# A rewritten beginning: the first image fetched on three queues ahead of the weights, its norm by matrix products, and the first strip's values first

## The chip, the cores and the metric

The kernel runs on one core of one Trainium2 chip. A core has five engines with a queue of instructions each: TensorE (PE; its weight loads are shown apart as PEld), VectorE (DVE), ScalarE (ACT), GpSimd (POOL) and SyncE (SP). SyncE, ScalarE and GpSimd issue DMA transfers. The metric is the device time of one execution in microseconds; it is given as the median over runs.

## The reference

The input x holds 16 images of 56 x 56 tokens with 384 channels, in float32. Two layers are computed, each added to its input:

```
x = x + window_attention(group_norm(x))
x = x + depthwise_conv3x3(group_norm(x), sign of the clipped weights)

group_norm(v):  32 groups of 12 channels; mean and variance over height, width and the
                channels of a group, per image; (v - mean) / sqrt(var + 1e-5)
window_attention(x):
    roll x by (-3, -3); q, k, v = split(x @ w_qkv.T); 12 heads of 32
    windows of 7 x 7 = 49 tokens; score = q k / sqrt(32) + relative position bias
    mask across the rolled border in the last row and column of windows
    softmax over the 49 keys; out = attn v, then @ w_out.T + b_out; roll back
```

So every image needs its whole group norm before the first window of it can be computed.

## The kernel before, in words

An image is cut into 8 strips of 7 rows (NS = 8), a strip into 8 windows, and a unit is half a strip, 4 windows. There are 128 strips and 256 units. Channels lie on the 128 partitions, in three chunks (NC = 3). For a unit, `scores` (L527) makes the products of keys and queries in four banks of PSUM, `softmax` (L550) scales them and adds the bias, `exponential` (L573) takes the exponential, `add_up` (L604) sums over the keys with a product of ones, `attend` (L622) makes the products with the values, `invert` and `divide` normalize, and `project` (L662) makes the output product and adds the input. For the next strip, `value` (L483) and `query_key` (L471) make the products with the weights from the normalized input `xn`, which `normalize` (L460) writes on ScalarE. `turn` (L496) transposes blocks of the values on VectorE, and `by_key` (L505) carries them to their places with 16 DMAs on SyncE. The first product of `add_up` in a strip waits for these carries.

The order of the work on each engine is the order in which the program issues it. `all_units` (L985) is the loop over the units: in it, `heavy` gives the products for the next strip, and the list `side`, filled by `plan`, gives the work of other images with a due time in units: image b + 1 is loaded on GpSimd's queue during image b (`fetch_halves` L409, `turn_halves` L437, `arrange` L442), and the convolution of image b - 1 runs on VectorE.

The beginning is written out by hand (L1032 to L1060). It concerns image 0 only:

- `clear` (L133) zeroes the tails of the staging buffers on GpSimd. Two of the buffers are `xls`; four more are borrowed from the tiles `es`, `xn`, `vt`, `vq` (the list `spare`, L128).
- `fetch` (L371) loads a strip by 6 DMAs (12 for the last strip, which wraps around the image), all on SyncE's queue. A token's 384 channels are one row of 1536 bytes. The strip's two parities of rows are fetched apart, and each of them as 48, 5 and 3 tokens, because of the roll. Strips 0 to 5 go to the six buffers at once, strips 6 and 7 to `xls` again when these are free.
- `fetch_weights` (L154) loads `w_qkv` and `w_out` by 12 DMAs on ScalarE's queue, at the same time.
- `load_bias` (L192) gathers the relative position bias by 49 row DMAs on GpSimd's queue, 38 of them early and 11 after the norm's power, then a copy of the rows and two DMAs of the mask.
- `load` (L386) transposes a strip on TensorE, ScalarE copies it into `xs`, and VectorE takes its statistics. `load_weights` (L163) transposes 3 x 3 blocks of a weight (n = 0 query, 1 key, 2 value, 3 output); of its three copies out of PSUM two are on VectorE, one on ScalarE. Weights 0, 1 and 2 are turned after strips 3, 5 and 7.
- `norm_gather` (L240) aggregates the statistics per channel, writes them to DRAM and reads them back with a group on each partition; `clear_again` (L148) zeroes `es`, `xn`, `vt` and `vq` on VectorE; `norm_scale` (L255) folds the 12 channels of a group by small VectorE operations, takes the power -0.5 on GpSimd (L281), writes to DRAM and reads the coefficients back per channel.
- The output weight, `load_depthwise` (L173, the sign of the convolution's weights by six operations and a transpose) and `add_bias` (L221, sixteen additions of bias and mask) follow, then `normalize(0)` and `all_units`, which begins with the first strip's queries and keys, scores, softmax, values, turns and carries.

The norm of the last image's second layer is another function, `norm_late` (L323): there the means over a group are products with the matrix `gmat` (seven of its 128 x 128 blocks), which `fetch_late` loads.

If a value leaves its range, a second, slower pass is computed (`tc.If(redo != 0)`); it is not entered with these inputs.

Of the kernel before, what the change touches and what calls it, by code (L numbers as in the profile page):

```python
# [9 lines left out]
F32 = mybir.dt.float32  # L10
# [8 lines left out]
EPS = 1e-5  # L19
# [15 lines left out]
def kernel(  # L35
# [97 lines left out]
    def clear():  # L133
        for xl in xls:
            nc.gpsimd.memset(xl[:, NL - 1, :], 0.0)

        for t in spare:
            nc.gpsimd.memset(t[:, NL - 1, :], 0.0)

    def clear_more():  # L140
        nc.gpsimd.memset(power, -0.5)
        nc.gpsimd.memset(ones, 1.0)
        nc.gpsimd.memset(least, LEAST)
        nc.gpsimd.memset(seen, 0.0)
        for t in (qk[:, :, ST:], *hps, *accs):
            nc.gpsimd.memset(t, 0.0)
# [5 lines left out]
    staged = []  # L152

    def fetch_weights():  # L154

        rows = [w[r * P : (r + 1) * P, :] for w in (w_qkv, w_out) for r in range(w.shape[0] // P)]
        for n in range(0, len(rows), NC):
            wl = xpool.tile([P, NC, ST], F32, tag="x", name=f"wl_{n}")
            for k in range(NC):
                nc.scalar.dma_start(wl[:, k, :C], rows[n + k])  # L160
            staged.append(wl)
# [10 lines left out]

    def load_depthwise():  # L173
        wl = [accs[1].rearrange("p h w -> p (h w)")[:9, n * C : (n + 1) * C] for n in range(3)]
        nc.scalar.dma_start(wl[0], w_dw.rearrange("a b c o -> (a b) (c o)"))
        for c in range(NC):
            nc.scalar.dma_start(bo_sb[:, c : c + 1], b_out[c * P : (c + 1) * P].unsqueeze(1))

# [144 lines left out]
    def norm_late(b):  # L323
        st, gm = stats.pop((1, b)), late_tiles["gm"]
        mv = small.tile([P, NC, 2], F32, tag="mv", name="mv_late")
        for c in range(NC):
            nc.vector.bn_aggr(mv[:, c, :], st[:, c].rearrange("p s k -> p (s k)"))
        nc.vector.tensor_tensor(mv[:, :, 0], mv[:, :, 0], bo_sb, ALU.add)
# [17 lines left out]
        mean = group_mean(mv[:, :, 0], "pg_mean")  # L346
        dev = small.tile([P, 3, NC], F32, tag="dev_late", name="dev_late", bufs=1)
# [4 lines left out]
        var = seen[:, B : B + NC]  # L352
        nc.vector.tensor_scalar(var, group_mean(dev[:, 0], "pg_var"), EPS, None, ALU.add)
        nc.gpsimd.tensor_tensor(dev[:, 1], var, power.to_broadcast([P, NC]), ALU.pow)
        coef = small.tile([P, NC, 2], F32, tag="coef", name="coef_late", bufs=4)
        nc.vector.tensor_copy(coef[:, :, 0], dev[:, 1])
        nc.vector.scalar_tensor_tensor(coef[:, :, 1], dev[:, 2], -1.0, dev[:, 1], ALU.mult, ALU.mult)
        coefs[1, b] = coef

    xs = {}

    def staging(s):

        if NS > s >= 2 and s < 2 + len(spare) and staged:
            return spare[s - 2]
        return xls[s % 2]

    def fetch(s):  # L371
# [3 lines left out]
        for odd in range(2):  # L375
            t, end = 0, (WIN + 1 - odd) // 2
            while t < end:
# [4 lines left out]
                for lo, hi in ((SHIFT, SHIFT + 48), (SHIFT + 48, W), (W, R)):  # L382
                    nc.sync.dma_start(here[lo - SHIFT : hi - SHIFT], rows[lo % W : (hi - 1) % W + 1])
# [495 lines left out]
    def plan_last(b, first):  # L879
# [6 lines left out]
        at(first, norm_late, b)  # L886
# [98 lines left out]
    def all_units(fast):  # L985
        for m in range(2 * NC):
            query_key(0, m)
        scores(0, fast)
        softmax(0, fast)
        for m in range(NC):  # L990
            value(0, m)
        normalize(1)
        exponential(0, fast)
        for m in range(NC):
            turn(0, m)
        by_key(0)
# [35 lines left out]
    with tc.manual_schedule():  # L1032
        nc.scalar.preload_act_table_set("natural_log_exp_and_others")
        clear()
        nc.vector.memset(score_banks, 0.0)
        staged.append(None)
        for s in range(2 + len(spare)):
            fetch(s)
        staged.clear()
        fetch_weights()  # L1040
        clear_more()
        load_bias(nc.gpsimd, 0, 38, True)
        for s in range(NS):
            for c in range(NC):
                load(s, c)
            if s + 2 + len(spare) < NS:
                fetch(s + 2 + len(spare))
            if s % 2 and s > 1:
                load_weights(s // 2 - 1)
        norm_gather((0, 0), nc.sync)  # L1050
        clear_again()
        for xl in xls:
            nc.gpsimd.memset(xl, 0.0)
        norm_scale((0, 0), nc.sync, nc.vector)
        load_bias(nc.gpsimd, 38, T, True)
        load_weights(NC)
        load_depthwise()
        add_bias(True)
# [81 lines left out]
```

## Time and profile before

| what | us |
|---|---|
| median of 3 runs | 4051.73 (4049.64 to 4053.24) |
| the profiled execution's own time | 4050.03 |
| its span, first to last instruction | 4048.2 |
| TensorE busy | 3948.1 (98%) |
| VectorE busy | 3495.5 (86%) |
| ScalarE busy | 2227.4 (55%) |
| GpSimd busy | 1858.7 (46%) |
| last strip of image 0 lands (its transposes start) | 39.49 |
| its last statistics end | 42.89 |
| first query product starts | 59.38 |
| products with the values of unit 0 end | 94.67 |

The profile is one execution. "L474" is line 474 of the program. A line of the timeline or the chain begins with the start and the length in microseconds; a group names its engine, its line and its tiles, written from read, and at the end the idle time of the engine before it and what ended that. "PEclk" is the clock granted to TensorE as a share of full speed. DMA share is the mean busy share of the core's 16 DMA engines. The span is 1.8 us shorter than the execution's own time.

### The profile page before, as it was taken

How to read it: one execution, taken by the hardware profiler on the slowest of the kernel's cores; microseconds unless marked ns; L12 is line 12 of the kernel's file. 1: busy time of each engine (PE TensorE's matmuls, PEld its weight loads, DVE VectorE, ACT ScalarE, POOL GpSimd, SP SyncE). 2: the span in 40 equal slices, each digit the busy share in tenths (PEclk: the TensorE clock that was granted, in tenths of full speed). 3: DMA queues.
4: the chain of work that ended last, by engine and by line, in shares of the span. 5: the costliest groups of instructions: out<-in, count | busy, mean ns of one | idle time of the engine just before them, and what ended most of it. 6: DMA issues, size and time to landing. Idle time of an engine off the chain costs nothing.

```text
span 4048.2 us, 144624 instructions
## 1 busy us (share of the span) xinstructions
PE 3948.1 (98%) x63161; PEld 2408.9 (60%) x63161; DVE 3495.5 (86%) x3712; ACT 2227.4 (55%) x4654; POOL 1858.7 (46%) x3165
## 2 busy tenths in 40 slices
PE   5999999999999999999999999999999999999987
PEld 3656555555566565555655656565555556556657
DVE  4555989889898998989889898998989899898897
ACT  2545655555565655655555565655556556565552
POOL 5444535545463554545446453554545455452100
PEclk8999999999999999999999999999999999999998
DMA  3323445454554554445454454554545454553444
GB/s 96 81 60 93 112 101 128 109 113 98 120 115 112 118 117 104 114 99 128 108 117 109 111 118 106 118 119 101 118 101 123 106 126 104 112 120 80 114 100 107
DMA packets 803093, 438.90 MB, mean 108 GB/s; under 512 B 672538, under 2 KB 753083, under 8 KB 802450
## 3 DMA queue, kind: packets, MB, share of 16 engines
q1 hardware_dynamic: 711784, 267.66, 30.4%
q0 software_dynamic: 87648, 159.12, 15.7%
q8 instruction: 498, 8.16, 0.9%
q10 hardware_dynamic: 3018, 2.78, 0.3%
q14 instruction: 145, 1.19, 0.1%
HBM read 169.63 MB, written 158.46 MB: 81 GB/s over the span
## 4 chain that ended last, share of the span: by engine, by line
PE 33%; issue 22%; POOL 18%; DVE 16%; DMA 8%; ACT 2%; SPq 1%; DVEq 0%; ACTq 0%; POOLq 0%
POOL xl L421 13%; PE pq L474 13%; PE pv L487 7%; PE py L671 7%; DVE o L799 6%; PE score_banks L541 2%; PE po L632 2%; DMA mvd<-mv 2%; DVE xt L438 2%; DVE e L558 2%; DMA xl<-in_x_dram 2%; PE score_banks L611 1%; POOL dev L270 1%; SPq L511 1%; DMA cod<-both 1%
## 5 line engine op out<-in xcount | busy, mean ns | idle before, releaser
L474 PE MATMUL pq<-xn,wq_t 128*128 128x392 f32 x4608 | 1586.8, 497 | 0.2 <-issue 0.2
L421 POOL DMA_DIRECT2D xl<-in_x_dram x1980 | 1329.2, 729 | 143.9 <-DVE xt L438 96.9
L799 DVE SCALAR_TENSOR_TENSOR o<-hp,dw_t,o 128x1568 f32<-128x1568 f32 x752 | 1379.1, 1834 | 5.4
L474 PEld LDWEIGHTS pq<-xn,wq_t 128*128 128x128 f32 x4608 | 846.1, 188 | 596.2 <-issue 1.8
L487 PE MATMUL pv<-xn,wq_t 128*128 128x392 f32 x2304 | 814.6, 497 | 15.2 <-DVE y L679 14.0
L671 PE MATMUL py<-ot,wo_t 128*128 128x392 f32 x2304 | 817.6, 500 | 8.4 <-DVE ot L660 7.8
L481 ACT COPY qk<-pq 128x392 f32<-128x392 f32 x768 | 367.2, 482 | 565.6 <-PE pq L474 565.2
L691 POOL COPY y<-y 128x63 f32<-128x63 f32 x128 | 54.7, 427 | 1276.7 <-DVE y L679 1276.7
L487 PEld LDWEIGHTS pv<-xn,wq_t 128*128 128x128 f32 x2304 | 423.6, 188 | 314.9 <-DVE y L679 16.2
L671 PEld LDWEIGHTS py<-ot,wo_t 128*128 128x128 f32 x2304 | 424.8, 190 | 312.0 <-DVE ot L660 27.1
L576 ACT ACTIVATE e<-e 128x1176 f32<-128x1176 f32 x256 | 303.3, 1185 | 495.9 <-DVE e L558 494.8
L652 DVE SCALAR_TENSOR_TENSOR ln<-score_banks,inv 128x588 f32<-128x588 f32 x256 | 196.0, 766 | 321.7 <-ACT inv L651 317.6
L494 ACT COPY vt<-pv 128x392 f32<-128x392 f32 x384 | 188.8, 492 | 367.6 <-PE pv L487 366.8
L558 DVE SCALAR_TENSOR_TENSOR e<-score_banks,bias 128x1176 f32<-128x1176 f32 x256 | 347.3, 1357 | 8.7 <-PE score_banks L541 8.7
L541 PEld LDWEIGHTS score_banks<-qk 32*49 32x49 f32 x24576 | 265.8, 118 | 145.9 <-issue 113.0
L632 PEld LDWEIGHTS po<-e,v 49*32 49x32 f32 x24576 | 311.8, 105 | 58.7 <-issue 8.2
L450 ACT COPY x<-xt 128x196 f32<-128x196 f32 x720 | 225.6, 368 | 180.8 <-DVE xt L438 180.7
L632 PE MATMUL po<-e,v 49*32 49x49 f32 x24576 | 311.0, 212 | 7.2 <-DMA v<-vq 7.0
L541 PE MATMUL score_banks<-qk 32*49 32x49 f32 x24576 | 298.2, 218 | 3.1 <-DVE ln L652 3.0
L498 DVE STREAM_TRANSPOSE vq<-vt 128x512 f32<-128x512 f32 x384 | 266.1, 694 | 8.6 <-ACT vt L494 5.5
L463 ACT ACTIVATE xn<-x,coef 128x392 f32<-128x392 f32 x384 | 247.0, 711 | 13.2 <-DMA coef<-cod 13.2
L679 DVE TENSOR_TENSOR y<-py,x 128x392 f32<-128x392 f32 x384 | 213.6, 556 | 42.1 <-PE py L671 41.6
(174 smaller groups left out, 3281.7 us busy)
## 6 DMA issues: line engine op xcount, KB each, us to landing
v<-vq SPq DMA_DIRECT2D x2048, 48.0 KB
xb<-mid SPq DMA_DIRECT2D x90, 855.5 KB
out_dram<-o SPq DMA_DIRECT2D x736, 98.0 KB
mid<-y POOLq DMA_DIRECT2D x112, 619.5 KB
xl<-in_x_dram POOLq DMA_DIRECT2D x1260, 52.5 KB
mid<-y POOLq DMA_DIRECT2D x15, 354.0 KB
xl<-in_x_dram POOLq DMA_DIRECT2D x180, 28.0 KB
mid<-y POOLq DMA_DIRECT2D x15, 265.5 KB
```

The source lines that it names most:

```text
L421: nc.gpsimd.dma_start(xz[i * D + lo : i * D + hi, c, k : k + n, :], flat[token : token + n * (hi - lo)].rearrange("(k t) c -> t k c", k=n) ...
L463: nc.scalar.activation(xn[:, c, :, :T], xs[s][:, c, :].rearrange("p (w t) -> p w t", t=T), AF.Identity, bias=coef[:, c, 1:2], scale=coef[: ...
L474: nc.tensor.matmul(pq[:, :ST].rearrange("p (w t) -> p w t", t=T), wq_t[:, c, m * P : (m + 1) * P], xn[:, c, :, :T], start=(c == 0), stop=( ...
L481: nc.scalar.copy(qk[:, m, :ST], pq[:, :ST])
L487: nc.tensor.matmul(pv[:, :ST].rearrange("p (w t) -> p w t", t=T), wq_t[:, c, 2 * C + m * P : 2 * C + (m + 1) * P], xn[:, c, :, :T], start= ...
L498: nc.vector.transpose(vq[:, :, :, m].rearrange("p h n d -> p n h d"), vt[:, m].rearrange("p (n w) (j b) -> p n (w j) b", w=2, b=D),)
L541: nc.tensor.matmul(pp[row * HT : row * HT + rows, i, k0 : k0 + T], qk[part, NC * fast + j, q0 : q0 + rows], qk[part, NC * (not fast) + j, ...
L558: nc.vector.scalar_tensor_tensor(e, pp[:, :, : NC * 2 * T].rearrange("q i (n k) -> q i n k", k=T), QSCALE, bias[:, int(s % NS == NS - 1)]. ...
L576: nc.scalar.activation(flat, flat, AF.Exp, accum_out=reach[:, 0, u : u + 1])
L632: nc.tensor.matmul(po[w][i * D : (i + 1) * D, (2 * j + r) * T : (2 * j + r + 1) * T], vs[s][keys, i, n * 2 + r, j], by_head(u)[keys, i * N ...
L671: nc.tensor.matmul(py[:, :ST], wo_t[:, c, m * P : (m + 1) * P], ots[s][:, c, :], start=(c == 0), stop=(c == NC - 1),)
L799: nc.vector.scalar_tensor_tensor(acc, by_half(hp[:, dy : dy + BR, dx : dx + W]), dw_t[:, c, t : t + 1], acc, ALU.mult, ALU.add)
```

## The change

It rewrites the beginning.

1. *Buffers and clears.* Two more staging buffers are borrowed from the tiles of `by_key` (`vpool`), so each of the eight strips has its own; the tails are cleared on VectorE (`make_room`). The clears of `es`, `xn`, `vq` and most of `vt` are gone; only the padding of `vt` is cleared, after the norm. The clears of `hps`, `accs` and `xls` move from early on GpSimd's queue to after the bias (`clear_conv`), since three of these hold weights first.
2. *Queues.* Strip 0 goes on ScalarE's queue, strips 1, 3, 5, 6 on SyncE's, strips 2, 4, 7 on GpSimd's. The group matrix follows on GpSimd's queue. The weights of value, query and key follow on SyncE's queue, then the convolution's weights and the output bias, then the output weight. GpSimd's small clears and bias rows come after the image; 22 rows are before the norm's power and 27 after it.
3. *Norm.* `norm_late` becomes `norm_products` and serves image 0 too. Between the products for the mean and the operation that reads them, the value weight is turned (`meanwhile`).
4. *Order.* All strips are loaded with no weights between. `normalize(0)` comes straight after the norm, then the query and key weights are turned, and `all_units` starts with values, turns and carries, then queries and keys; then the output weight, the convolution's weights, the bias and the clears; then scores and softmax.

```diff
-    def clear():
-        for xl in xls:
-            nc.gpsimd.memset(xl[:, NL - 1, :], 0.0)
-        for t in spare:
-            nc.gpsimd.memset(t[:, NL - 1, :], 0.0)
+    homes = {}
+    def make_room():
+        late = [vpool.tile([P, NL, C], F32, tag="v", name=f"xv_{n}") for n in range(2)]
+        for s, t in enumerate((*xls, *spare, *late)):
+            nc.vector.memset(t[:, NL - 1, :], 0.0)
+            homes[s] = t
...
-        for t in (qk[:, :, ST:], *hps, *accs):
-            nc.gpsimd.memset(t, 0.0)
+        nc.gpsimd.memset(qk[:, :, ST:], 0.0)
+
+    def clear_conv():
+        for t in (*hps, *accs, *xls):
+            nc.gpsimd.memset(t, 0.0)
...
+    def fetch_weights(n, home):
+        wl = home.rearrange("p a b -> p (a b)")[:, : NC * C].rearrange("p (k c) -> p k c", c=C)
+        for k in range(NC):
+            r = (NC * n + k) * P
+            rows = w_qkv[r : r + P] if n < NC else w_out[k * P : (k + 1) * P]
+            nc.sync.dma_start(wl[:, k], rows)
+        staged[n] = wl
...
+    def fetch_depthwise():
+        nc.sync.dma_start(
+            accs[1].rearrange("p h w -> p (h w)")[:9, :C], w_dw.rearrange("a b c o -> (a b) (c o)")
+        )
+        for c in range(NC):
+            nc.sync.dma_start(bo_sb[:, c : c + 1], b_out[c * P : (c + 1) * P].unsqueeze(1))
...
-    def norm_late(b):
-        st, gm = stats.pop((1, b)), late_tiles["gm"]
+    def norm_products(key, gm, meanwhile=None):
+        st = stats.pop(key)
...
-        mean = group_mean(mv[:, :, 0], "pg_mean")
+        mean = group_mean(mv[:, :, 0], f"pm{name}")
+        if meanwhile:
+            meanwhile()
...
-    def fetch(s):
+    def fetch(s, queue):
...
-                    nc.sync.dma_start(here[lo - SHIFT : hi - SHIFT], rows[lo % W : (hi - 1) % W + 1])
+                    queue.dma_start(here[lo - SHIFT : hi - SHIFT], rows[lo % W : (hi - 1) % W + 1])
...
-    def all_units(fast):
+    def all_units(fast, meanwhile=None):
+        for m in range(NC):
+            value(0, m)
+            turn(0, m)
+        by_key(0)
         for m in range(2 * NC):
             query_key(0, m)
+        if meanwhile:
+            meanwhile()
         scores(0, fast)
         softmax(0, fast)
-        for m in range(NC):
-            value(0, m)
         normalize(1)
         exponential(0, fast)
-        for m in range(NC):
-            turn(0, m)
-        by_key(0)
...
-        clear()
+        make_room()
         nc.vector.memset(score_banks, 0.0)
-        staged.append(None)
-        for s in range(2 + len(spare)):
-            fetch(s)
-        staged.clear()
-        fetch_weights()
+        for s, queue in enumerate((nc.scalar, nc.sync, nc.gpsimd, nc.sync, nc.gpsimd, nc.sync, nc.sync, nc.gpsimd)):
+            fetch(s, queue)
+        gm = bpool.tile([P, BR + 2, R], F32, tag="xb", name="gm_first").rearrange("p h w -> p (h w)")
+        pairs = len(group_blocks(C, GS))
+        gm = gm[:, : pairs * P].rearrange("p (n q) -> p n q", q=P)
+        nc.gpsimd.dma_start(gm, gmat)
+        for n, home in ((2, hps[0]), (0, hps[1]), (1, accs[0])):
+            fetch_weights(n, home)
+        fetch_depthwise()
         clear_more()
-        load_bias(nc.gpsimd, 0, 38, True)
+        load_bias(nc.gpsimd, 0, 22, True)
         for s in range(NS):
             for c in range(NC):
                 load(s, c)
-            if s + 2 + len(spare) < NS:
-                fetch(s + 2 + len(spare))
-            if s % 2 and s > 1:
-                load_weights(s // 2 - 1)
-        norm_gather((0, 0), nc.sync)
-        clear_again()
-        for xl in xls:
-            nc.gpsimd.memset(xl, 0.0)
-        norm_scale((0, 0), nc.sync, nc.vector)
-        load_bias(nc.gpsimd, 38, T, True)
-        load_weights(NC)
-        load_depthwise()
-        add_bias(True)
+        fetch_weights(NC, xpool.tile([P, NC, ST], F32, tag="x", name="wl_out"))
+        norm_products((0, 0), gm, lambda: load_weights(2))
+        load_bias(nc.gpsimd, 22, T, True)
         normalize(0)
-        all_units(True)
+        for n in range(2):
+            load_weights(n)
+        nc.vector.memset(vt[:, :, :, T:], 0.0)
+        homes.clear()
+        def meanwhile():
+            load_weights(NC)
+            load_depthwise()
+            add_bias(True)
+            clear_conv()
+        all_units(True, meanwhile)
```

## The prediction, made before the changed kernel was run

> **What bounds the kernel now.** I read the page first (busy shares, then the forty slices), next a table of stretches, then the chain that ended last over the first 220 us, then the DMA queues of single stretches, and last the norm at the kernel's end, which is built as the new beginning is.
>
> ```profile
> span 4048.2 us, 144624 instructions
> PE 3948.1 (98%) x63161; PEld 2408.9 (60%) x63161; DVE 3495.5 (86%) x3712; ACT 2227.4 (55%) x4654; POOL 1858.7 (46%) x3165
> PE   5999999999999999999999999999999999999987
> ```
>
> TensorE is full in every slice but the first and the last two. In the stretches (start and end, length, then busy time of PE, PEld, DVE, ACT, POOL, clock, DMA share, GB/s) the holes end at 94.7 us:
>
> ```profile
> 16.00:40.00 24.00, 16.52 (x105) 15.25 (x106) 13.39 (x25) 11.20 (x23) 16.42 (x31) 0.97 0.66 161
> 40.00:59.40 19.40, 6.05 (x33) 5.58 (x32) 14.82 (x38) 3.29 (x7) 6.76 (x12) 0.59 0.05 3
> 59.40:94.70 35.30, 26.80 (x269) 15.16 (x269) 11.10 (x23) 10.52 (x21) 19.68 (x30) 0.84 0.28 65
> 94.70:124.60 29.90, 29.90 (x403) 17.57 (x409) 14.27 (x19) 13.79 (x32) 1.51 (x3) 0.96 0.12 28
> ```
>
> From 94.7 us TensorE sets the pace, with work that the change leaves alone. So the change is worth what it moves the end of the first unit's products with the values (94.67 us), one for one. The chain shows what sets that end (start, length, what):
>
> ```profile
> 39.49 2.24 PE pl L396 x12
> ...
> 50.18 1.34 DVE vq L150
> ...
> 58.92 0.46 PE pdw L187 x3
> 59.38 13.73 PE pq L474 x36
> 73.11 1.07 PE score_banks L541 x74
> 74.18 6.14 PE pv L487 x18
> ...
> 91.44 1.91 DMA v<-vq
> 93.40 1.27 PE po L632 x78
> 94.67 5.22 PE pv L487 x12
> ```
>
> The last strip lands at 39.4; the norm with its two trips through DRAM and the clears of L150 holds the first query product until 59.38; after the values the sixteen carries of L511 (81.6 to 93.4) hold the attention.
>
> **What limits the image's arrival.** Between 16 and 36 us SyncE loads alone, beside tiny rows of the bias. Queue view of that stretch (packets, MB, share of 16 engines):
>
> ```profile
> q1 hardware_dynamic: 2561, 3.48, 68.1%
> ```
>
> The strips land about 3.35 us apart (the tensor engine starts on them at 16.04, 19.28, 22.50 ... 39.49), at 68% of the engines. The Trainium skill (DMA: Bandwidth & Descriptors, "Why a DMA increments its semaphore by 16 and not by 1") says that a transfer is spread over the largest number up to 16 that divides its slowest dimension, on the lowest-numbered engines if SyncE or ScalarE issues it, from a rotating start if GpSimd does. A strip has pieces of 48, 5 and 3 tokens by 7 rows: 21 rows for each engine, 7 more on engines 0 to 4, 7 more on 0 to 2. The lowest three carry 35 rows, the mean is 24.5: 70%, and the trace's 68.1% agrees. One row costs the full engine 3.35/35 = 0.096 us. Check on the whole load before: 280 image rows x 0.096 = 26.9, and twelve weight transfers x 8 rows at 0.087 (281 GB/s in 5 to 10 us, when ScalarE's queue had 98% of the engines) = 8.4; with the start at 1.3 that is 36.6, the trace says 39.4, so 2.8 us are latency and gaps. The same page ("Issuing engines are not separate DMA queues") says that queues interleave on the same 16 engines; the trace agrees where ScalarE's weights hold SyncE's strips back (SyncE waited 8.5 us for them).
>
> **The change, part by part.**
>
> *Image ahead of weights, three queues.* Strips 0, 1, 3, 5, 6 stay on hardware queues: 5 x 35 = 175 rows on the lowest engine. GpSimd's three add 3 x 24.5 = 73.5 if their small pieces rotate. 248.5 x 0.096 = 23.9. Start 1.7 (VectorE starts at 1.24 and clears the tail first, 0.4 us, as POOL's equal memset at L135 took) + 23.9 + 2.8 = 28.4 instead of 39.4. Bounds: 23.3 if all rows spread evenly (196 rows, 18.8 us), 31.4 if GpSimd's pieces use the low engines too (280). GpSimd issues 24 image transfers and the group matrix at 0.5 to 0.7 each (L210, L421), 15 us: not the limit. Each strip's transposes (2.24) fit between arrivals. Tail: 39.49 to the last statistics at 42.89 is 3.4, and since strip 7 is behind strip 6 on TensorE but comes by another queue, 0 to 2.2 more; I take 1.1. Statistics end at **32.9, not 42.9**: -10.0.
>
> *Norm by products.* The late norm has all the pieces, and there the clock was slow after a short idle:
>
> ```profile
> 3957.40 3.12 PE L337 MATMUL pg_mean<-mv_late,gm 128*128 128x1 f32 x14 [2.28 <-DVE mv_late L328]
> 3961.45 3.12 PE L337 MATMUL pg_var<-dev_late,gm 128*128 128x1 f32 x14 [0.93 <-DVE dev_late L351]
> 3964.85 0.90 POOL L354 TENSOR_TENSOR dev_late<-seen,power 128x3 f32<-128x3 f32 x1 [8.81 <-DVE seen L353]
> ```
>
> Aggregates 0.8 + 0.1; mean 3.1; then, on the path, nine weight transposes 2.1 (28.66 us) and their last copy 0.7, since VectorE's queue has both copies ahead of the mean; four small operations 0.8; variance 3.4 with its wait; addition, power and coefficients 1.4: 12.4. Three normalizing activations 1.9 end at 14.3; the other eighteen transposes (4.05 at 41.53) run from the variance's end beside them, the last held by VectorE's copies; first value product at 14.6. That is 32.9 + 14.6 = **47.5**; before, 42.9 to 59.4 was 16.5: -1.9. Gone are 6.4 us of clears, four DMAs and seventeen small VectorE operations; added is most of that in slow products. The Trainium skill (TensorE: Matmul & The Clock Gate, "What's actually happening") says that the array runs at half clock until some 3.4 us of sustained work; the trace shows both (twelve transposes 2.24 at 16 us, 1.24 at 33.6). Warm, this part is about 4 us shorter. The power on GpSimd stands behind 22 bias rows; from about 24 at 0.65 each (30 rows from 10.66 to 30 us, waits within) they end at 38, power is asked for at 43: hidden, at most 3 us if the image's issues drag.
>
> *Values first.* Nine groups now run at a stretch; the first query group took 3.8, later ones 1.97: 3.8 + 8 x 1.97 = 19.6, or 17.7 warm; after four us of transposes I take 18.6, to 66.1. The carries start some 9 us in, take 10 on SyncE and 2 to land: about 69, hidden by the query and key products and by what follows; uncovered they would cost 12 as before.
>
> *What is late next.* Depthwise taps and bias, hidden before under the norm and the queries, now follow the last query: nine output-weight transposes 1.2, copy 0.65, six operations 2.8 (56.0 to 58.8), turn 0.6, tap copy 0.3, bias
>
> ```profile
> 65.87 5.86 DVE L230 TENSOR_TENSOR bias<-rel,mask 128x147 f32<-128x147 f32 x16 [6.26 <-DMA mask<-in_wmask_dram]
> ```
>
> then score addition 1.4, exponential 1.4, sums and attention 1.75: 16.1. Behind the waiting transpose on TensorE stand the scores, but they finish under the bias. So 66.1 + 16.1 = **82.2, not 94.7**: first product to this point 34.7 against 35.3, -0.6. Value-first frees the carries' wait and the bias takes its place.
>
> *Off the path.* GpSimd's later clears (two of 1.5, two of 1.55, two of 1.4) put its loads for image 1 from 64 to about 75; twelve take 8.5, so strip 8 lands near 86 and is turned near 101 (19 us after the first attention, as before). Memsets beside VectorE's bias cost nothing by the Trainium skill (SBUF, "Who interferes with whom": a two-input VectorE instruction contends with GpSimd's reads, not its writes); no stretch of before shows that pair, so up to 1 us. Weights land behind strip 6, 8 rows an engine each, before they are used.
>
> Sum: -10.0 - 1.9 - 0.6 = **-12.5 us**; profiled span 4048.2 to 4035.7, its device time 4050.0 to 4037.5; on the median of the runs shown, 4051.7 to **4039**.
>
> **Rivals.** (a) *Evenly spread and warm*: landing 23.3, statistics 27, value product 10.5 later, 17.7 + 16.1: 71; -23, 4028. For it: TensorE has been working in bursts; against: it stayed slow from 16 to 30 us with this same rhythm. (b) *Low engines stay crowded and all is slow*: landing 31.4, weights mixed with GpSimd's strips 2, power 1 late, 19.6 for the groups: 82.2 + 6 = 88 to 89; -6, 4045.5. For it: GpSimd's rotation is seen in no stretch here. (c) *Slower: the bias waits for GpSimd.* From mask landing to the first attention are 10.5 us, so it decides beyond a landing at 84. Expected: power at 43, 27 rows x 0.51, duplicate and masks 4, landing 2: 63. If GpSimd's image loads wait for one another until 60 instead of 25, the mask lands near 95 and the time is 11 longer: 4063. Against it: 24 loads of 52.5 KB (L421, from 64.0 us) went at 0.70 each. (d) *Nothing won*: the first product waits for the weights now queued behind the image; that needs them 12 us later than the image, and they are 72 rows, 6.3 us.
>
> **How the numbers follow.** The main case has 0.50 (own range 4034 to 4043), (a) 0.22, (b) 0.22, (c) 0.04, (d) 0.02. A change of this kernel can be told from none at about 0.2%, 8 us: faster below 4043.6. All of the main case and (a) and half of (b) lie there: 0.83; the other half and (d) within: 0.13; slower 0.04. Range 4029 to 4047: it reaches into (a) and past (b).
>
> **What would show it.** Right: the last image transfer lands at 27 to 31; the statistics end near 33; the product with the group matrix takes 3.1 each; the first value product starts at 44 to 49; a hole of some 8 us in TensorE under the bias; attention ends near 82, and strips of 29.9 us follow. Wrong: landing at 23 or beyond 34, GpSimd's power waiting, the bias released by a DMA, or a strip of image 1 late at its turn.

## The result and the profile after

The changed kernel takes 4041.5 us in the median of 13 runs (4038.74 to 4046.88), the kernel before 4052.55 us in 13 runs beside it (4049.64 to 4054.47). The ratio is 0.9974 with a 95% interval of 0.9965 to 0.9982: faster by 0.26%, 11.0 us. The forecast was 4039 with a range of 4029 to 4047.

The profiled execution took 4039.94 us. Its page begins as before's did; TensorE is still full in every slice but the first and the last two:

```profile
span 4038.0 us, 144675 instructions
PE 3952.3 (98%) x63189; PEld 2414.4 (60%) x63189; DVE 3493.3 (87%) x3706; ACT 2229.6 (55%) x4654; POOL 1891.9 (47%) x3184
PE   6999999999999999999999999999999999999987
```

The same four stretches as before the change (start and end, length, busy time of PE, PEld, DVE, ACT, POOL, clock, DMA share, GB/s):

```profile
16.00:40.00 24.00, 16.57 (x102) 15.70 (x100) 13.99 (x27) 11.90 (x24) 15.42 (x35) 0.81 0.87 202
40.00:59.40 19.40, 18.00 (x74) 14.31 (x74) 6.70 (x17) 4.62 (x9) 13.73 (x27) 0.71 0.07 13
59.40:94.70 35.30, 26.55 (x371) 16.59 (x370) 17.10 (x33) 10.01 (x20) 29.74 (x40) 0.85 0.28 60
94.70:124.60 29.90, 29.90 (x490) 18.00 (x489) 15.72 (x22) 15.27 (x35) 8.88 (x15) 1.00 0.28 70
```

The hole of 13.4 us in the second stretch is nearly gone (18.00 busy instead of 6.05), but much of what fills it is slow products of the norm. The third stretch, where the carry stood, has as much idle time as before: 8.75 us against 8.50. Something else stands in the carry's place. The chain of waits says what (start, length, what):

```profile
26.12 6.61 DMA xv<-in_x_dram
...
32.87 4.26 PE pl L409 x24
...
38.63 3.12 PE pm L347 x14
...
45.17 3.12 PE pv L347 x14
...
51.84 6.02 PE pv L500 x18
57.86 11.85 PE pq L487 x36
...
71.28 1.15 DVE o L187
...
75.72 3.03 DVE bias L238 x9
...
85.56 1.24 PE po L645 x85
86.79 5.18 PE pv L500 x12
```

The last strips land at 32.87 instead of 39.49, the statistics end at 38.26 instead of 42.89, the first value product starts at 51.69, the last query group ends at 69.71, the bias is added from 75.72 to 81.5, and the attention of unit 0 ends at 86.79 instead of 94.67. No carry is in the chain any more: the depthwise weights (L187 to L196) and the bias (L238) are what the scores wait for.

At that point 7.9 us are won. The span is 10.2 us shorter, the median 11.0 (the interval of the ratio is 7.3 to 14.2 us, so 7.9 lies in it). To see where the rest comes from, I read one more mark, the start of the sums of unit 8 (L611 before, L624 after): 213.78 before, 205.93 after, again 7.9. The other 2.3 us of the span fall after unit 8. They are discussed at the end of the next section.

### The profile page after: what moved, and what is told of

It is laid out like the page before. It is cut to its first block, busy times and chain, and to the rows that moved or that the text cites. A ratio compares the mean times of both kernels' runs of the same rounds, so it can differ in the third digit from the quotient of the medians.

```text
span 4038.0 us, 144675 instructions
## 1 busy us (share of the span) xinstructions
PE 3952.3 (98%) x63189; PEld 2414.4 (60%) x63189; DVE 3493.3 (87%) x3706; ACT 2229.6 (55%) x4654; POOL 1891.9 (47%) x3184
## 4 chain that ended last, share of the span: by engine, by line
PE 41%; issue 18%; POOL 16%; DVE 15%; DMA 8%; ACT 2%; SPq 1%; DVEq 0%; POOLq 0%; ACTq 0%
PE pq L487 16%; POOL xl L434 11%; PE pv L500 8%; PE py L684 8%; DVE o L812 6%; PE score_banks L554 3%; PE po L645 2%; DMA xl<-in_x_dram 2%; PE score_banks L624 2%; DVE e L571 2%; DMA mvd<-mv 1%; DVE xt L451 1%; POOL dev L278 1%; DMA gt<-mvd 1%; DVE st L467 1%
## 5 line engine op out<-in xcount | busy, mean ns | idle before, releaser
L500 PE MATMUL pv<-xn,wq_t 128*128 128x392 f32 x2304 | 815.5, 497 | 13.4 <-DVE y L692 13.4
```

Source lines behind the costliest of these rows:

```text
L500: nc.tensor.matmul(pv[:, :ST].rearrange("p (w t) -> p w t", t=T), wq_t[:, c, 2 * C + m * P : 2 * C + (m + 1) * P], xn[:, c, :, :T], start= ...
```

## The experiments

The sum of the prediction had four terms: the image arrives by the rows on the busiest engines; the norm's products cost a known time; values first frees the carry; the bias takes the carry's place. Three of them hold to 1.2 us or better, and the arrival was too early by 5.4 us. So the experiments ask two things: what sets the arrival, and whether values first and the late bias are worth what the sum said. Ratios are against the kernel before on the same chip, whose median was 4052.77 (36 runs), 4051.79 (27 runs) and 4052.7 (17 runs) in the three groups of runs. A diff is against the changed kernel unless another is named. In the table, the first product and the sums of unit 8 are starts in TensorE's timeline, the end of the attention is read from the chain of waits.

| kernel | median us | ratio (95%) | first product of unit 0's strip | attention of unit 0 ends | sums of unit 8 start, against 213.78 before |
|---|---|---|---|---|---|
| changed kernel | 4041.5 | 0.9974 (0.9965 to 0.9982) | 51.69 | 86.79 | -7.9 |
| one queue | 4040.76 | 0.9969 (0.9956 to 0.9981) | 50.70 | 86.02 | -7.5 |
| small pieces on GpSimd | 4045.85 | 0.9985 (0.9978 to 0.9992) | 54.03 | 88.93 | -5.5 |
| whole rows, three queues | 4039.22 | 0.9968 (0.9957 to 0.9980) | 48.56 | 83.39 | -10.3 |
| whole rows, one queue | 4037.43 | 0.9964 (0.9949 to 0.9978) | 47.52 | 82.78 | -10.7 |
| norm through DRAM | 4046.23 | 0.9987 (0.9980 to 0.9994) | 53.35 | 89.79 | -4.7 |
| queries first | 4050.17 | 0.9993 (0.9984 to 1.0002) | 50.88 | 97.91 | +4.4 |
| queries first, clears later | 4049.02 | 0.9992 (0.9984 to 1.0001) | 51.43 | 91.10 | -2.2 |
| bias first | 4036.83 | 0.9967 (0.9954 to 0.9979) | 51.02 | 80.88 | -12.1 |
| bias first, by SyncE | 4033.59 | 0.9958 (0.9944 to 0.9972) | 52.10 | 78.72 | -16.6 |
| all together | 4028.79 | 0.9943 (0.9930 to 0.9957) | 47.55 | 74.20 | -21.0 |

### What sets the arrival: one queue

```diff
-        for s, queue in enumerate((nc.scalar, nc.sync, nc.gpsimd, nc.sync, nc.gpsimd, nc.sync, nc.sync, nc.gpsimd)):
+        for s, queue in enumerate((nc.sync,) * NS):
```

> All eight strips on SyncE's queue, the rest as in the changed kernel. There strip 6 landed at 32.9 us, not at 28.4 as predicted. Theory A: the lowest DMA engines carry the small pieces of 5 and 3 tokens of every queue, GpSimd's too; then 280 rows x 0.096 us set the landing whatever the queues, and this kernel lands its last strip at 31 to 33.5 us, first attention (end of the products with the values of unit 0) at 85 to 88, total within 3 us of the changed kernel's 4041.5. Theory B: two queues at once raise the price of a row for each other (packets took 0.13 us instead of 0.07), so one queue is no worse: also 31 to 33. Theory C: the third queue does bring bandwidth, and without it the last strip lands at 36 us or later and the total rises by 3 to 6 us.

The last strip is transposed from 33.54 on, 0.7 later than with three queues, and the first value product starts at 50.70, 1.0 earlier; the time is the same. Three queues bring nothing here over one. Theories A and B both had that; the next run tells them apart. The DMA queues between 2 and 30 us show why (packets, MB, share of 16 engines). First the changed kernel:

```profile
q1 hardware_dynamic: 1897, 2.61, 50.4%
q0 software_dynamic: 1023, 1.80, 34.2%
q10 hardware_dynamic: 440, 0.60, 10.6%
```

then the kernel with one queue (its q0 has the bias rows and the group matrix, 0.51 MB at 9.0%):

```profile
q1 hardware_dynamic: 3201, 4.37, 68.5%
```

The share is 95% with three queues and 77.5% with one, but 5.01 MB moved against 4.89 MB. What rose is the price of a packet. On SyncE's queue it is 0.504 x 16 x 28 / 1897 = 0.119 us with three queues and 0.685 x 16 x 28 / 3201 = 0.096 us with one. (The prediction's 0.096 is another measure, the time from strip to strip over 35 rows; by that, one queue has 0.099. The division of this paragraph gives 0.681 x 16 x 20 / 2561 = 0.085 for the prediction's stretch of the kernel before.) A packet is counted as under way while it shares its engine with another queue's, and so a high share is no sign of more data. The Trainium skill (DMA: Bandwidth & Descriptors, "Issuing engines are not separate DMA queues") says that several issuing engines save only the time of issuing; the two runs agree, 33.54 against 32.87.

With one queue, strip 0 is transposed from 9.3 on and the others 3.46 us apart on average, much as before the change. With three, strips 0 and 1 come together, at 15.5, and strips 6 and 7 together, at 32.87. So 24 transposes (4.26 us) follow the last landing instead of 12 (2.24), and that more than cancels the 0.7.

### Small pieces on GpSimd's queue

```diff
-                    queue.dma_start(here[lo - SHIFT : hi - SHIFT], rows[lo % W : (hi - 1) % W + 1])
+                    q = queue if hi - lo > 8 or b or not homes else nc.gpsimd
+                    q.dma_start(here[lo - SHIFT : hi - SHIFT], rows[lo % W : (hi - 1) % W + 1])
...
-        for s, queue in enumerate((nc.scalar, nc.sync, nc.gpsimd, nc.sync, nc.gpsimd, nc.sync, nc.sync, nc.gpsimd)):
+        for s, queue in enumerate((nc.scalar, nc.sync, nc.sync, nc.sync, nc.sync, nc.sync, nc.sync, nc.sync)):
```

> Pieces of 48 tokens on SyncE's and ScalarE's queues, all pieces of 5 and 3 tokens on GpSimd's queue. Theory A with a rotating start on GpSimd's queue: 8 x 21 rows plus 8 x 3.5 spread, 196 rows x 0.096 = 18.8 us, last landing at 24 to 27 us, total 5 to 8 us below the changed kernel. Theory A without rotation (GpSimd's small pieces use the low engines too): no change, 31 to 34. Theory B (queues slow each other): little change, 30 to 34.

It was worse than every branch: the last strips are transposed only from 36.37 on. The pieces of 48 tokens were not what was late, they had landed by 27.9. GpSimd's small ones waited for one another, up to 2.4 us at a time in the timeline of 20 to 40 us, and the last were issued only from 35.35 on. So the time is no test of whether GpSimd's small pieces rotate over the engines.

The trace is one, since it records when each DMA engine reports its share of a transfer. In the changed kernel, SyncE's piece of 48 tokens issued at 9.12 is reported by eleven engines from 14.74 to 15.45, by two at 17.0 and by three from 18.7 to 19.0. Five engines carry more, and three of them most, as the rule of the split has it for SyncE's and ScalarE's pieces of 5 and 3. With one queue the same five are seen in GpSimd's bias rows: those issued at 7.26 are reported by eleven engines from 10.14 to 10.68 and by five from 12.41 to 13.36. With the small pieces on GpSimd's queue no such group is left: its piece of 5 tokens issued at 9.21 is reported by all sixteen from 17.36 to 18.13, and the sixteen reports of each SyncE piece of the image lie within 0.8 to 2.1 us of each other (1.1 to 5.9 in the changed kernel). So GpSimd's small pieces were spread over all engines. From 8 to 20 us, before any weight is issued, the queues were (packets, MB, share) first with one queue, then with the small pieces on GpSimd's:

```profile
q1 hardware_dynamic: 1435, 1.97, 74.4%
q0 software_dynamic: 566, 0.04, 4.7%
```

```profile
q1 hardware_dynamic: 1494, 2.10, 97.9%
q0 software_dynamic: 403, 0.21, 12.8%
```

SyncE's queue keeps nearly all sixteen engines at work now, and yet 2.31 MB moved in these 12 us instead of 2.01. A packet on SyncE's queue takes 0.979 x 16 x 12 / 1494 = 0.126 us instead of 0.744 x 16 x 12 / 1435 = 0.100. The rows are spread as the main case of the prediction had it, and the price of a row takes most of the gain, as theory B had it. It also shows once more what a share is: from 2 to 32 us the DMA engines have a share of 1.08, which cannot be work done one after another.

### Whole rows: 28 rows on the busiest engine instead of 35

```diff
+                if homes:
+                    queue.dma_start(here, rows)
-                for lo, hi in ((SHIFT, SHIFT + 48), (SHIFT + 48, W), (W, R)):
+                for lo, hi in () if homes else ((SHIFT, SHIFT + 48), (SHIFT + 48, W), (W, R)):
...
+        to = xs[s][:, c, :].rearrange("p (w r c) -> p r w c", r=WIN, c=WIN)
+        if homes:
+            rows = pt[:, :ST].rearrange("p (r j) -> p r j", j=W)
+            whole = (NW - 1) * WIN
+            nc.scalar.copy(to[:, :, : NW - 1], rows[:, :, SHIFT : SHIFT + whole].rearrange("p r (w c) -> p r w c", c=WIN))
+            nc.scalar.copy(to[:, :, NW - 1, : WIN - SHIFT], rows[:, :, SHIFT + whole :])
+            nc.vector.tensor_copy(to[:, :, NW - 1, WIN - SHIFT :], rows[:, :, :SHIFT])
```

All 56 tokens of a row parity go in one DMA, and the roll is made in the copies out of PSUM. By the rule of the prediction, 56 tokens are split over 14 engines: 4 tokens of 7 rows, 28 rows on each, where the three pieces put 35 on the lowest three.

> Each strip part is fetched as 56 tokens in one DMA instead of 48, 5 and 3, and the roll by 3 columns is made by the copies out of PSUM (two on ScalarE, one small one on VectorE). 56 splits over 14 engines, so 28 rows of a strip on each instead of 35 on the busiest. Theory A: 224 rows x 0.096 = 21.5 us, last landing at 26 to 28, first attention 4 to 6 us earlier than 86.8, total 4035 to 4038. Theory B (bytes and mutual slowing set the time): landing 31 to 33, total 4040 to 4043. A third of the DMAs also means fewer waits in the queues; if the issue limits, it gains without the engines, which the landing cannot tell apart but the run with the small pieces on GpSimd's queue can.

Strip 6 is transposed from 29.34 on, 3.5 earlier than in the changed kernel, and the attention of unit 0 ends 3.4 earlier, at 83.39. The same with every strip on SyncE's queue:

> The run with whole rows of 56 tokens, but all strips on SyncE's queue. Theory A (crowding of the lowest engines: 28 rows a strip on the busiest instead of 35): against the run with all strips on SyncE (last strip's transposes at 33.5) 56 rows x 0.096 = 5.4 us earlier, 28 us; DMA share during the load up from 0.76 to about 0.88. With theory B on top (queues slow each other) it lands no later than the three-queue run with whole rows (29.3 for strip 6). Rival (bytes alone set the rate, or the issue does): 33 or unchanged against the one-queue run if bytes; if the third queue is what helped whole rows, 31 or later. Total 4035 to 4038 under A.

There the last strip is transposed from 29.91 on instead of 33.54: 3.6 earlier, where 5.4 was expected. From the first strip's transposes to the last's are 33.54 - 9.3 = 24.2 us in pieces and 29.91 - 8.0 = 21.9 us whole. Per strip and row of the busiest engine that is 24.2 / 7 / 35 = 0.099 and 21.9 / 7 / 28 = 0.112 us. So the rows of the busiest engines do matter, and fewer of them bring the image sooner, but the price of a row rises as more engines are used: a cut of the rows by a fifth shortens this part by a tenth. Between 8 and 20 us SyncE's queue shows the same:

```profile
q1 hardware_dynamic: 1609, 2.30, 93.2%
```

A packet takes 0.932 x 16 x 12 / 1609 = 0.111 us, between the 0.100 in pieces (share 74.4%) and the 0.126 with all engines at work (97.9%), and all queues together moved 194 GB/s, against 167 and 192. One queue alone did this, so it is not the number of queues. What holds the image near that rate stays open; the weights of the kernel before went at 295 GB/s from 5 to 10 us.

The expectation named a rival: a third of the DMAs also wait less for one another at the queue. The trace of the one queue in pieces speaks against it. From 8 to 31 us at least three engines have a packet of SyncE's queue under way in 99% of the time, so the three busiest hardly pause for an issue.

### The norm through DRAM again

```diff
-        norm_products((0, 0), gm, lambda: load_weights(2))
+        norm_gather((0, 0), nc.sync)
+        load_weights(2)
+        norm_scale((0, 0), nc.sync, nc.vector)
```

> The changed kernel with the old norm for image 0 (aggregate, DRAM, folds, DRAM), without the old clears and with the value weight turned between. Theory A (prediction: the products save about 2 us): the old norm took 14.4 us from aggregates to coefficients at its place in the kernel before, the new one 11.6 with nine transposes in it; first value product at 53 to 54 instead of 51.7, first attention 88 to 89, total 4043 to 4044. Rival B (the products are the change's main gain): later by 5 us or more. Rival C (the DMAs were slow only beside the weights; now they are quick): no difference or a gain.

VectorE waits for the statistics to come back from DRAM:

```profile
45.37 0.16 DVE L281 COPY dev<-gt 32x12 f32<-32x12 f32 x1 [6.46 <-DMA gt<-mvd]
```

From the aggregates to the first value product are 16.1 us instead of 13.5, so the products are worth 2.6 us. There is a second part: the value products then take 8.41 us instead of 6.16, and the ten us before had little work for TensorE; I put it down to the array being slower after a pause, which was not tested apart (with queries first, below, they took 8.09 soon after a wait of 8.70). The attention of unit 0 ends 3.0 later, where theory A had 1 to 2. The median gains 5.6 us on the kernel before instead of 11.0; the intervals are too wide to tell A from B by the time.

### Values first: undone, with and without the clears beside it

```diff
     def all_units(fast, meanwhile=None):
-        for m in range(NC):
-            value(0, m)
-            turn(0, m)
-        by_key(0)
...
         softmax(0, fast)
+        for m in range(NC):
+            value(0, m)
         normalize(1)
         exponential(0, fast)
+        for m in range(NC):
+            turn(0, m)
+        by_key(0)
```

> The first strip's order as before: queries and keys, then output weight, depthwise, bias, scores, softmax, then values, turns and carries; the rest as in the changed kernel. Theory A (prediction's reading: the bias takes the carries' place): queries 51.7 to 64, bias from 70 (mask lands) to 76, softmax to 77, turns behind it to 79, carries 79 to 90, landing 92, first attention ends 93 to 94, so 6 to 7 us later than 86.8, total about 4048. Rival B: value-first brings the whole carry wait of 12 us: attention at 98 to 99, total about 4053. Rival C: it brings nothing, since the bias is last either way: 86 to 88, total about 4042.

The attention of unit 0 ended at 97.91, which looks like the larger theory. But VectorE's timeline of this kernel has a line that no theory had in it (start, length, instruction):

```profile
64.84 0.57 DVE L188 TENSOR_SCALAR o<-o 9x384 f32<-9x384 f32 x1
65.35 5.43 DVE L189 TENSOR_SCALAR o<-o 9x384 f32<-9x384 f32 x1
```

The same instruction in the changed kernel:

```profile
72.73 0.34 DVE L189 TENSOR_SCALAR o<-o 9x384 f32<-9x384 f32 x1
```

GpSimd's timeline at that moment of the kernel with queries first:

```profile
65.98 3.05 POOL L151 MEMSET hp<- 128x1740 f32 x2
68.96 1.61 POOL L151 MEMSET o<- 128x1792 f32 x1
```

VectorE's scaling ends as the clears end, 0.2 us after them. It began 0.6 us ahead of them, while GpSimd was still issuing the mask's transfers, and by its usual 0.34 it would have been done; what held it in between is not shown. It lies on the path to the values, because the transpose of the depthwise weights and then the scores and values stand behind it on TensorE. So the order was tried again with the clears of the convolution's buffers in units 2 and 3 (diff against the kernel just shown):

```diff
     def clear_conv():
-        for t in (*hps, *accs, *xls):
+        for t in xls:
             nc.gpsimd.memset(t, 0.0)
+        for n, t in enumerate((*hps, *accs)):
+            at(2.1 + 0.4 * n, nc.gpsimd.memset, t, 0.0)
```

> Queries and keys first, as in the run before that had values second, but GpSimd's clears of the four convolution buffers (4.5 us) are moved from the beginning to units 2 and 3, so that they no longer run beside VectorE's first scaling of the depthwise weights, which took 5.43 us there instead of 0.34. Theory A (that run lost 5 us to GpSimd's clears, and values first is worth 6 us, the part of the carry's 12 us that nothing else covers): attention of unit 0 ends at 92.5 to 93.5, time 4046 to 4047. Theory B (the carry of the values alone sets the end there, and values first is worth all of its 10 us): attention ends at 96.5 to 98, time 4050. The moved clears cost nothing in the steady part under both; if they did, both times would be 1 to 4 us higher with the attention's end as given.

The three scalings take 0.35 us each, and the chain goes through the carries to the attention:

```profile
85.67 3.24 DMA v<-vq
88.95 2.15 PE po L647 x87
91.10 6.36 PE pv L502 x12
```

The attention of unit 0 ends at 91.10, earlier than either theory had it, and the sums of unit 8 start at 211.59: 6.6 earlier than with the clears in the way, 5.7 later than in the changed kernel. That is the 6 us of theory A for values first: less than half of the carry's 12, since the bias takes the place. The time is nearer to B: 4049.0 where A said 4046 to 4047. By unit 8 the order had lost 5.7 against the changed kernel, in the medians it has lost 7.4 (a gain of 3.7 on the kernel before instead of 11.0). The difference is within the scatter that is described below; whether the clears in units 2 and 3 cost some of it was not measured apart. The gain of the profiles does not show fully in the medians of the two runs either (4050.17 and 4049.02, one with and one without the stretch); the profile of the first is at the slow side of its runs, so the stretch need not happen in each execution.

### The bias ahead of the output weights and the depthwise weights

```diff
         def meanwhile():
-            load_weights(NC)
-            load_depthwise()
             add_bias(True)
             clear_conv()
+        def afterwards():
+            load_weights(NC)
+            at(0.4, load_depthwise)
+            at(1.4, turn_depthwise)
+            at(1.45, nc.gpsimd.memset, accs[1], 0.0)
-        all_units(True, meanwhile)
+        all_units(True, meanwhile, afterwards)
```

`afterwards` is called behind the first softmax, `turn_depthwise` is the transpose and copy at the end of `load_depthwise`, and the clear of `accs[1]`, which holds the depthwise weights, follows it.

> The bias additions come straight after the first strip's turns; the output weight is turned after the first softmax and the depthwise weights during units 0 and 1. Theory A (the bias chain behind the last query is the bound): the additions start when the mask lands, about 69.6 us (GpSimd's last mask DMA ends at 67.6 in the changed kernel), so first attention at 80 to 81 instead of 86.8, total about 4035. Rival (TensorE's idle time there is set by something else, such as the carries or the second strip's norm): within 1 us of the changed kernel.

The attention of unit 0 ends at 80.88, as expected, 5.9 earlier than in the changed kernel. Now the bias does wait for a transfer:

```profile
69.81 5.86 DVE L241 TENSOR_TENSOR bias<-rel,mask 128x147 f32<-128x147 f32 x16 [11.43 <-DMA mask<-in_wmask_dram]
```

So the last 27 rows of the bias were next, with SyncE fetching them instead of GpSimd:

```diff
-        load_bias(nc.gpsimd, 22, T, True)
+        load_bias(nc.sync, 22, T, True)
```

> As the run with the bias first, and the last 27 rows of the bias, their copy and the mask go on SyncE's queue, which is idle from 39 to 59 us. Theory A: mask lands at 58 to 61, the additions end at 65 to 67, before the last query product; the first attention then follows queries, scores, softmax and exponential: 75.5 to 77 us, total about 4031. Rival (the carries, now behind the rows on SyncE, become the bound): attention held by a DMA at 78 or later.

The bias starts at 67.05 and the attention of unit 0 ends at 78.7, some 2 to 3 us later than expected. SyncE issued the 27 rows from 39.26 on, at 20.11 / 27 = 0.74 us each where GpSimd needs 0.50, so they were ready no earlier than 62. And the clears came earlier on GpSimd's queue, where two of them (L151, 3.02 us from 47.63 on) met VectorE's copies of the coefficients:

```profile
47.58 3.10 DVE L371 COPY coef<-dev 128x3 f32<-128x3 f32 x1 [1.01 <-POOL dev L369]
```

The copy took 3.10 instead of 0.17 us, and the first value product, which needs the coefficients, started at 52.10 although the products for the mean had started 1.9 us earlier than in the changed kernel (36.71, 38.63). The late bias was not what stood last: its additions ended at 72.9, and the chain to the attention goes through the queries, which ended at 71.00, and ScalarE's normalization of the next strip (1.93 from 73.33 on) ahead of the exponential.

### All together

Whole rows on SyncE's queue, the bias first, 36 of its 49 rows ahead of the power and 13 behind it, all on GpSimd, and the clears after the mask, those of `xls` first. Diff against the kernel with whole rows on one queue, beside the one of the bias above:

```diff
-        load_bias(nc.gpsimd, 0, 22, True)
+        load_bias(nc.gpsimd, 0, 36, True)
...
-        load_bias(nc.gpsimd, 22, T, True)
+        load_bias(nc.gpsimd, 36, T, True)
```

> All that the runs so far point to, together: every strip on SyncE in whole rows of 56 tokens with the roll made in the copies; 36 of the 49 rows of the relative bias are fetched by GpSimd ahead of the power instruction and 13 behind it; the bias is added right after the query and key products are issued; output weights and depthwise weights are turned after the first softmax. Theory A (the first unit waits for the last of arrival, products and bias in turn, and what each was late adds up): last strip at 30, first value product at 47.5, last query group at 65.5, bias ended before it, attention of unit 0 ended at 72 to 73, which is 10 before the same kernel with the late bias (82.7); time 4037.4 - 10 = 4027 (4025 to 4030). Theory B (the gains of arrival and of the bias overlap, because the values' carry by 32 transfers or the last rows of the bias then take the wait): attention at 77 to 80, time 4031 to 4035.

4028.79 us, ratio 0.9943 (0.9930 to 0.9957): faster than before by 0.57%, 23.9 us, where the changed kernel gained 11.0. VectorE has the bias done under the queries:

```profile
57.74 5.86 DVE L241 TENSOR_TENSOR bias<-rel,mask 128x147 f32<-128x147 f32 x16 [1.81 <-POOL xl L151]
```

and the chain of waits stays on TensorE from the value products nearly to the attention:

```profile
47.76 6.90 PE pv L510 x18
54.65 11.85 PE pq L497 x36
...
68.92 1.93 ACT xn L486 x3
...
72.84 1.36 PE po L655 x69
74.20 4.15 PE pv L510 x12
```

Both gains add up, as theory A said. The 1.2 to 2.2 us by which the attention is later than its 72 to 73 are 1.0 in the query groups, which end at 66.50 rather than 65.5, and ScalarE's normalization of the next strip, 1.93, which now stands ahead of the exponential on the path.

### What stays open

In every kernel of the table the median gains more than the beginning does: 11.0 against 7.9 in the changed kernel, 23.9 against 21.0 in the last. It is 0.9 to 4.5 us, and 7.0 with queries first. Most of that lies in the yardstick: the marks of the kernel before, 213.78 among them, come from one execution of 4050.03 us, and its medians beside these runs are 1.8 to 2.7 us above it. When each profiled span is set against the 4048.2 of that execution, the part after unit 8 is 2.3 us shorter in the changed kernel and 1.8 in the last, but 0.9 longer in both kernels with one queue and 1.5 with the norm through DRAM. Over all eleven it lies between 3.1 longer and 3.4 shorter, 0.5 shorter on average. The 13 runs of the changed kernel alone range over 8.1 us. So the surplus needs no cause in the steady part, and none is seen. What stays open is what limits the image's rows when all engines are at work.

## Why the prediction was right, and where it was off

The forecast was 4039, the time is 4041.5, faster by more than the bound of 0.2%, as the main case had it. By its steps:

- *What bounds the kernel.* From the end of unit 0's attention on TensorE sets the pace, and the beginning counts one for one. The stretch from 94.7 to 124.6 us is full after the change too, and the medians of the other kernels follow the beginning, from 2 to 21 us earlier, but for the 0.9 to 4.5 us above; the one with queries first is the exception (its profile is the slowest of its runs).
- *The image ahead of the weights, three queues: statistics at 32.9.* This is the step that failed: they end at 38.26. The landing was put at 28.4 and is 32.87, beyond even the upper bound of 31.4. The tail after it was put at 4.5 and is 5.4, since the last two strips land together. The mis-sized term is the price of a row, 0.096 us, read at a share of 68% of the engines and used at 95%: 32.87 less the 4.5 of start and latency, over the 248.5 rows of the sum, is 0.114. The rotation of GpSimd's pieces, on which the sum was based, was there (the small pieces on GpSimd's queue were spread over all engines), and it brought next to nothing, since rows that are spread better cost more each, 0.126 us with all engines at work. So the advantage of three queues, 28.4 against 31.4, was not there: with one, the 280 rows at 0.099 land 0.7 later. GpSimd's issues of the image, put at 15 us, ended at 26.7, since they waited up to 2.25 us for earlier transfers to land; SyncE's ended no sooner (26.4), so they were not the limit alone.
- *The rows on the lowest engines.* The whole rows agree with the Trainium skill's rule of the split ("Why a DMA increments its semaphore by 16 and not by 1") in direction: 28 rows on the busiest engines instead of 35 are 3.5 and 3.6 us sooner. The price per row isn't constant, 0.099 and 0.112, and a sum in rows at one price overstates the gain.
- *The norm by products, 14.6.* It took 13.4 from the statistics' end to the first value product. The product with the group matrix took 3.12 twice, as the late norm showed; the way through DRAM costs 2.6 more, where -1.9 was put against before.
- *Values first, nine groups in 18.6.* They took 18.0. The carries are hidden. From the first product to the attention's end are 35.1 us against 35.3 before, where 34.7 was forecast: the carry's wait is freed and the bias takes its place. Queries first without the clears' stretch confirms the size, 5.7 by unit 8.
- *What is late next, 16.1.* It took 17.1, and 0.9 of the difference is one instruction: L187 took 1.22 us, beside GpSimd's clear of `o` from 70.60 to 72.21, where L188 takes 0.35. The bias is the right successor: moving it and the depthwise weights gives 5.9 us, and fetching it earlier the rest.
- *Clears beside VectorE's bias cost nothing.* Right for the bias, which takes 5.86 us beside them as before; the instructions ahead of it, of which the prediction said nothing, were held. The Trainium skill (SBUF, "Who interferes with whom") says both: a two-input VectorE instruction contends only with GpSimd's reads, and copies and scalings can take the pair of ports that GpSimd uses, and then one blocks the other. The prediction used the first of these alone. The runs show both: additions, and copies out of PSUM, at their usual length beside the clears, a scaling and a copy within SBUF held until they end.

Of the rivals, the one in which the low engines stay crowded (landing 31.4, attention at 88 to 89, 4045.5) is nearer to the beginning as measured, 32.87 and 86.79, but not for its reason, since GpSimd's pieces did not crowd the low engines. The time lies between the two, because 2.3 us of the profiled span fall after unit 8, which no step had and which is within the scatter there. That part of the closeness is luck. The evenly spread and warm case is excluded. The case of the bias waiting for GpSimd did not happen here, its mask transfers were issued by 67.64; it became the next limit only when the bias was moved ahead.

The sum again with what was measured: arrival and tail +5.4, norm -1.2, groups -0.6, what is late next +1.0; 4.6 in all, and 82.2 + 4.6 is the 86.8 of the trace.

## What to carry to other kernels

Read the price of a transfer's row where as many DMA engines work as will after the change; here a second and a third queue brought no data sooner, since a row's price rose with the engines at work, while pieces that divide evenly over more engines brought it 3.5 us sooner, less than the count of rows promised. When a wait is freed, list what else the next step needs and move that too: here the change won 11 us, and moving what stood in the freed wait's place, with better pieces, won some 13 more. A large GpSimd clear is to be kept away from VectorE's copies and scalings within SBUF on the path, also when it looks as if nobody waited for it; beside the additions of the bias it cost nothing.

## What was not expected of the hardware

- GpSimd's clears held a VectorE scaling and a copy from SBUF to SBUF until they ended: the scaling of 9 x 384 took 5.43 us instead of 0.34, the copy of 128 x 3 3.10 instead of 0.17. Having one input is not what decides it: copies out of PSUM (L176) took their 0.56 us beside clears, statistics (L403) 0.57 and a transpose (L514, with the bias by SyncE) 0.71, and the additions of two inputs their 5.86.
- The busy share of the DMA engines exceeds one: 1.08 over 30 us with three queues at work, while 204 GB/s moved. The whole rows on three queues moved 229 GB/s at a share of 1.00.
- A row of the image costs a DMA engine more when more engines are at work: 0.100 us at a share of 74%, 0.111 at 93%, 0.126 at 98% of SyncE's queue.
- The eighteen value products took 8.41 us instead of 6.16 in the kernel in which ten us with little work stood ahead of them.
